# Later stages, an earlier fetch of weights and a shifted unit in a two-layer convolution and attention kernel

## The chip, the cores and the metric

The kernel runs on one core of a Trainium2 chip. The metric is the device time of one execution in microseconds (us), lower is better; the time of a kernel is the median of its runs. Beside the timed runs there is one profiled execution, from which the trace and the profile come.

## The reference

Two layers act on an image batch `x` of shape (2, 256, 64, 64), all in float32. In short:

```
# layer 0
q, k, v = 1x1 convolutions of x, 8 heads of 32 channels, 4096 tokens an image
fuse    = softmax(q k^T / sqrt(32)) v              # per head, 4096 x 4096
hybrid  = Wf [x, fuse] + bf                        # 1x1 convolution
x       = hybrid * m + x * (1 - m)                 # m: mask, resized bilinearly
# layer 1
x = x * sigmoid(relu(x ca_w1 + b) ca_w2 + b)       # channel gate
x = x + window_attention(x)                        # 8x8 windows, 4 heads of 64
x = shuffle of the channels (4 groups)
y = relu(bn(conv7x7(x, groups=64)))                # 256 -> 64 channels
y = bn(conv7x7(y, groups=64))                      # 64 -> 256 channels
out = x * sigmoid(y)
```

The full attention of layer 0 is most of the arithmetic. The two grouped 7x7 convolutions need whole rows around each pixel, so they can begin for an image only when enough of its rows have come out of layer 1's window attention.

## The kernel before

**Preparation.** A first part projects q, k and v chunk by chunk and puts them into DRAM. It is not touched.

**Attention in slots.** `pipeline` walks over 1024 slots: image `b` (2), chunk `c` of 512 query tokens (8), half of the heads `g` (2) and block `m` of 128 keys (32). A chunk is therefore 64 slots. In slot `i` the loop emits the scores of slot `i + 2` (TensorE, L643), which ScalarE turns into exponentials in a tile `e` (L656, eight buffers, `EB = 8`), and the products of slot `i` with v (TensorE, L695). VectorE adds every `e` tile into a running sum (L701), from which the softmax denominators come later. A tile `e` is free again when its product and its sum are done.

**Denominators.** At the last slot of each half, all chunks before the last two ("folded" chunks) have their sums added up across partitions by accumulating DMAs on GpSimd's queue (`fold`, L673). Some slots after the end of a chunk, `at(delay, action)` emits: a few matmuls (`dna`, L729) and a copy (`inva`, L736), a reciprocal on VectorE (L756), a store of the reciprocals to DRAM (`invs`, L741), a broadcast load of them to all partitions (`rda`, L748) and last the multiplication of the attention's result (`fa`, L762). For a folded chunk these stand 10, 11, 11, 11 and 17 slots behind the chunk's last slot; for the last two chunks 8, 9, 9, 9 and 15.

**Stages.** The rest of layers 0 and 1 up to the convolutions is the generator `stage(b, c)`, in 13 pieces. Each piece is emitted after a slot whose number is a multiple of four, while the attention of the next chunk runs. The pieces, in order: `hy` (L529, the 1x1 convolution over x and over `fa`), `ca1` and `ca2` (channel sums and gate), projection `qk0`, window scores `sc0`, `qk1`, `sc1`, `v`, the normalising, `pt` (transposes), `o`, `op` (output projection), and last `xo` (L1009) with the row stores `xs` (L1024) into DRAM, which go through GpSimd's queue, behind the folds and ahead of the next chunk's `invs`. The stage is put into the list of stages 17 slots behind a folded chunk (29 for the very first), so `hy` comes after slot 16 of the next chunk, in program order right behind `fa`; 16 slots behind an unfolded one.

**The tail.** After the last slot the last chunk's denominators and stage remain, and the convolutions. The convolutions are the generator `convolve`: 26 items, each a unit `u` of channels (16) and one or both images. An item has a first half `conv1` (L1093) and a second half `conv2` (L1118), then `gate` (L1145, VectorE) and twelve stores to the output per image (L1172), spread over the queues of GpSimd and SyncE. Rows `xea`, `xla` come by `load_rows` (L1072) and weights `wa` by `load_w` (L1065), both on SyncE's queue. Weights of units 1 to 8 live in the eight `e` buffers, so a load waits until attention has given the buffer back. The first nine items belong to image 0 and can be run before the last stage is done; item 9 is the first one that needs rows of image 1 and so the last stage's `xs`. `convolve` yields after each half, and the tail's loop advances it by one half wherever a piece of the last stage ends with `yield True`:

```
        while stages:
            if run_stages():
                next(conv)
```

So the order of TensorE's work in the tail is written out by the yields. In the kernel before it is: conv1(0), conv1(1), dna, conv2(0), conv1(2), conv2(1), hy, conv1(3), ca1, ca2, conv2(2), qk0, conv1(4), sc0, qk1, conv2(3), sc1, v, conv1(5), pt, conv2(4), o, conv1(6), op, conv2(5), conv1(7), conv2(6), conv1(8), conv2(7), conv1(9), and then halves alone. Nothing is planned by costs[...].

Of the kernel before, what the change touches and what calls it, by code (L numbers as in the profile page):

```python
# [17 lines left out]
B, C, H, W = 2, 256, 64, 64  # L18
# [4 lines left out]
NCHUNK = N // CH  # L23
# [7 lines left out]
EB = 8  # L31
DN = 8
# [25 lines left out]
def conv_seq_kernel(ctx: ExitStack, tc: tile.TileContext, a, out):  # L58
# [14 lines left out]
    def psum2(name):  # L73
        return ps["pair"].tile([P, 2, CH], F32, tag="s", name=name)
# [458 lines left out]
    def pipeline(arm, shifted, pools):  # L533
# [20 lines left out]
        es, acc, first, totals = {}, {}, {}, {}  # L554
        now = [0]
        later = deque()
        stages = deque()

        def at(delay, action):
            later.append((now[0] + delay, action))  # L560
# [13 lines left out]
        def load_q(b, c):  # L574
            q = qp.tile([P, KC, CH], F32, tag="q", name=f"q{arm}_{b}_{c}")
            nc.sync.dma_start(q, q_s[b, c].rearrange("p (g n) -> p g n", g=KC))
            qts[b, c] = q
# [188 lines left out]
        def stage(b, c):  # L766
# [45 lines left out]
                    )  # L812
            gt = gp.tile([P, half], F32, tag="g", name=f"g{tag}")
            nc.scalar.activation(gt, s[:, 0, 0:half], AF.Relu, bias=cb1)
            yield
            s = psum2(f"ca2{tag}")
            for oc in range(KC):
                for h in range(2):
# [219 lines left out]
        def convolve():  # L1038
# [17 lines left out]
            def load_w(u):  # L1056
                if u >= NU:
                    return
                n = 2 * 32 * UW
                if u == 0:  # L1060
                    t = cpool.tile([P, n], F32, tag="w0", name=f"w{arm}{u}")
                else:
                    t = ep.tile([P, HG, CH], F32, tag="e", name=f"w{arm}{u}")
                    t = t.rearrange("p h n -> p (h n)")[:, 0:n]
                nc.sync.dma_start(t, w_s[u])  # L1065
                ws[u] = t

            def load_x(k):
                u, images = items[k]
                x = xs[k] = early[k % 4] if k < EARLY else xcs[(k - EARLY) % len(xcs)]  # L1070
                for i, b in enumerate(images):
                    nc.sync.dma_start(  # L1072
                        x[:, nb * i : nb * i + nb].rearrange("p n g w -> p n (g w)"),
                        x_s[b, :, :, UG * u : UG * u + UG, :].rearrange("n p g w -> p n (g w)"),
                    )

            def load_rows(k):

                while len(xs) < min(k + 1, len(items)) and (
                    staged or B - 1 not in items[len(xs)][1]  # L1080
                ):
                    load_x(len(xs))

            def conv1(k):
                if k >= len(items):
                    return
                u, images = items[k]
                n = nb * len(images)
                w = ws[u][:, 0 : 32 * UW].rearrange("p (m g d) -> p g d m", g=UG, d=KS)
                s = psum1(f"c1{arm}{k}")  # L1090
                for d in range(KS):
                    for j in range(4):
                        nc.tensor.matmul(  # L1093
                            s[32 * j : 32 * j + 32, 0 : n * W],
                            w[:, j, d, :],
                            xs[k][:, 0:n, j, d : d + W],
                            start=(d == 0),
                            stop=(d == KS - 1),
                        )
                y = ys[k] = ycs[k % 2]  # L1100
                nc.scalar.activation(
                    y[:, 0:n, PAD : PAD + W],
                    s[:, 0 : n * W].rearrange("p (n x) -> p n x", x=W),
                    AF.Relu,
                    bias=cbias1[:, u : u + 1],
                )
# [34 lines left out]
            def gate(k, zs):  # L1141
                u, images = items[k]
                for m in range(len(images)):
                    x = xs[k][:, nb * m : nb * m + nb, :, PAD : PAD + W]
                    nc.vector.tensor_mul(zs[m], zs[m], x.rearrange("p n g x -> p g n x"))  # L1145

            def store(k, zs):
                u, images = items[k]
                engines = (nc.gpsimd, nc.gpsimd, nc.sync)
                if k == len(items) - 1:  # L1150
                    engines = (nc.scalar, nc.sync)
                elif k == len(items) - 2:
                    engines = (nc.scalar, nc.sync, nc.sync)
                elif k == len(items) - 3:
                    engines = (nc.gpsimd, nc.sync, nc.sync)
                elif len(images) == 2:
                    engines = (nc.gpsimd, nc.sync)
                stores = 0
                for m, b in enumerate(images):
                    for n, (x0, r0, r1) in enumerate(BLOCKS):  # L1160
                        for i in range(4):
                            p = 32 * i + 1 - x0
                            stores += 1
                            args = (
                                dst[b, i, r0:r1, UG * u : UG * u + UG, :],
                                zs[m][p + r0 : p + r1, :, n, :],
                            )
                            eng = engines[stores % len(engines)]
                            if eng is nc.scalar:
                                held.append(lambda a=args: nc.scalar.dma_start(*a))  # L1170
                            else:
                                eng.dma_start(*args)  # L1172
                if k == len(items) - 1:
                    while held:
                        held.popleft()()

            def more():
                if staged and not xcs:

                    for n in range(3):  # L1180
                        t = ep.tile([P, HG, CH], F32, tag="sum", name=f"xl{arm}{n}", bufs=3)
                        t = t.rearrange("p h n -> p (h n)")[:, 0 : B * nb * UG * WP]
                        xcs.append(t.rearrange("p (n g w) -> p n g w", n=B * nb, g=UG, w=WP))
                    xcs.append(pool.tile([P, B * nb, UG, WP], F32, name=f"xl{arm}3"))
                    for n in (2, 0):
                        xcs.append(room[:, n : n + 2].rearrange("p k n g w -> p (k n) g w"))
                    load_rows(EARLY)
                return bool(xcs)
# [2 lines left out]
            load_rows(3)  # L1191
            load_w(0)
            pool = yield
            for _ in range(4):
                load_w(weights.popleft())
            conv1(0)
            yield
            for k, (u, images) in enumerate(items):
                while len(xs) <= k + 1 < len(items):
                    if not more():  # L1200
                        yield
                conv1(k + 1)
                yield
                more()
                z = conv2(k)
                yield
                more()
                gate(k, z)
                if xcs:
                    load_rows(min(len(xs) + (k >= EARLY - 1), k + len(xcs)))  # L1210
                elif k + 4 < EARLY:
                    load_rows(k + 4)
                store(k, z)

                if weights and (weights[0] <= 1 + EB or k >= EARLY + 4):
                    load_w(weights.popleft())

# [8 lines left out]
        def run_stages():  # L1226
            while stages:
                waits = next(stages[0], stages)
                if waits is not stages:
                    return waits  # L1230
                stages.popleft()
# [10 lines left out]
        for i, (b, c, g, m) in enumerate(slots):  # L1242
            now[0] = i
            if (b, c, g, m) == (B - 1, NCHUNK - 1, 0, 12):
                for _ in banded:
                    pass
                conv = convolve()
                next(conv)
            if m % PB == 0:
                load_piece(i // PB + AHEAD)  # L1250
            if g == KC - 1 and m == 0:
                nxt = (b, c + 1) if c + 1 < NCHUNK else (b + 1, 0)
                if nxt[0] < B:
                    load_q(*nxt)
            rest = scores(i + 2) if i + 2 < len(slots) else None
            products(i)
            if rest:
                rest()
            if g == KC - 1 and m == NMB - 1:
                late = EB + 4 if (b, c) == (0, 0) else 0  # L1260
                at(DN + 8 + ((b, c) < (B - 1, NCHUNK - 2)) + late, lambda b=b, c=c: stages.append(stage(b, c)))
            run_later()
            if i % 5 == 1:
                next(banded, None)
            if i % 4 == 0:
                run_stages()
# [102 lines left out]
```

## Time and profile before

| what | value |
|---|---|
| median of 3 runs (lowest, highest) | 2900.6 us (2898.96, 2902.66) |
| profiled execution, its own time | 2911.19 us |
| its span, from first to last instruction | 2909.3 us |
| TensorE busy | 2863.8 us, 98% of the span |
| VectorE busy | 2435.4 us, 84% |
| ScalarE busy | 2455.3 us, 84% |
| GpSimd busy | 569.1 us, 20% |
| mean share of the DMA engines in use | q1 28.6%, q0 12.2% |
| last product of attention | about 2690 us |
| last matmul of the last convolution | about 2895 us |

A view of the waits names for every engine and line what it waited for, how long in total, how often, and the longest single wait. The chain is the path of work and releases that ended last. A timeline lists the instructions of one engine with start, duration and count, and the idle time before them in brackets. "issue" stands where an engine was idle and no semaphore explains it.

### The profile page before, as it was taken

What the parts mean: (1) busy time and instruction counts of PE and PEld (TensorE: products, weight loads), DVE (VectorE), ACT (ScalarE), POOL (GpSimd) and SP (SyncE); (2) the same over time, 40 slices, a digit from 0 to 9 for tenths busy, and PEclk for the clock granted to TensorE, in tenths of its full rate; (3) what the DMA queues carried; (4) which work ended last, traced back from release to release, by engine and by line L of the source; (5) the groups of instructions that cost most, each with busy time, mean ns of one, the idle gap of its engine ahead of it and who ended that gap; (6) DMA issues with size and microseconds to landing.
All of it is one profiled execution on the core that took longest, in us unless ns stands there. A gap on an engine that the chain in (4) does not pass through costs nothing.

```text
span 2909.3 us, 85471 instructions
## 1 busy us (share of the span) xinstructions
PE 2863.8 (98%) x37002; PEld 827.4 (28%) x37002; DVE 2435.4 (84%) x1344; ACT 2455.3 (84%) x4145; POOL 569.1 (20%) x937
## 2 busy tenths in 40 slices
PE   8999999999999999999999999999999999999998
PEld 3551122222222222222222222222222222222675
DVE  4249999899999999998999999999999899999211
ACT  5569989898989898989989898989899898989433
POOL 8111111111111212121111011111212110000476
PEclk9999999999999999999999999999999999999999
DMA  8545433433253434353333324343435342232565
GB/s 253 209 163 189 146 89 76 94 82 89 65 101 79 105 77 105 79 95 86 82 92 79 88 68 98 78 97 78 100 82 97 82 88 78 67 113 88 137 197 134
DMA packets 245690, 305.65 MB, mean 105 GB/s; under 512 B 121208, under 2 KB 137772, under 8 KB 245048
## 3 DMA queue, kind: packets, MB, share of 16 engines
q1 hardware_dynamic: 200068, 231.51, 28.6%
q0 software_dynamic: 40464, 65.79, 12.2%
q8 instruction: 293, 4.80, 0.7%
q10 hardware_dynamic: 4772, 2.79, 0.3%
q14 instruction: 93, 0.76, 0.1%
HBM read 221.88 MB, written 66.39 MB: 99 GB/s over the span
## 4 chain that ended last, share of the span: by engine, by line
PE 89%; DMA 4%; POOL 2%; issue 2%; DVE 2%; ACT 1%; ACTq 0%; POOLq 0%; DVEq 0%
PE sa L643 34%; PE ava L695 33%; PE qka L529 4%; PE hya L529 3%; PE c1a L1093 2%; PE vwa L529 2%; PE opa L529 2%; PE c2a L1118 2%; PE v L475 2%; PE q L438 2%; PE k L438 1%; DMA xs<-xo 1%; POOL out_dram L1172 1%; DMA invs<-inva 1%; DMA folda<-suma 1%
## 5 line engine op out<-in xcount | busy, mean ns | idle before, releaser
L656 ACT ACTIVATE ea<-sa 128x512 f32<-128x512 f32 (+1 forms) x3072 | 2037.0, 746 | 51.5 <-PE sa L643 24.5
L643 PE MATMUL sa<-qa,ka 32*64 32x512 f32 x16384 | 1147.5, 613 | 1.5 <-ACT vst L483 1.2
L701 DVE TENSOR_TENSOR suma<-suma,ea 128x2048 f32<-128x2048 f32 x480 | 1096.4, 2284 | 5.7 <-ACT ea L656 0.5
L695 PE MATMUL ava<-ea,va 128*32 128x512 f32 x8192 | 1091.8, 605 | 1.0
L701 DVE TENSOR_TENSOR odda<-odda,ea 128x2048 f32<-128x2048 f32 x420 | 958.4, 2282 | 45.9 <-ACT ea L656 45.8
L673 POOL DMA_DIRECT2D folda<-suma x336 | 235.7, 903 | 1669.6 <-DVE suma L703 981.6
L643 PEld LDWEIGHTS sa<-qa,ka 32*64 32x64 f32 x16384 | 242.4, 129 | 786.2 <-ACT ea L656 716.3
L695 PEld LDWEIGHTS ava<-ea,va 128*32 128x32 f32 x8192 | 161.6, 108 | 834.9 <-issue 805.4
L1172 POOL DMA_DIRECT2D out_dram<-za x212 | 119.7, 573 | 58.7 <-DVE za L1145 31.8
L701 DVE TENSOR_TENSOR suma<-ea,ea 128x2048 f32<-128x2048 f32 x32 | 73.2, 2286 | 58.9 <-ACT ea L656 58.9
L529 PE MATMUL qka<-ua,qkv_w 128*32 128x512 f32 x1024 | 115.8, 592 | 0.1
L785 ACT ACTIVATE ta<-hya,bf 128x512 f32<-128x512 f32 x32 | 20.3, 684 | 100.6 <-PE hya L529 94.6
L1024 POOL DMA_DIRECT2D xs<-xo x94 | 72.3, 1058 | 139.6 <-DVE xo L1009 137.4
L457 DVE TENSOR_REDUCE top<-sq 128x128 f32<-128x2048 f32 x16 | 36.6, 2285 | 74.8 <-ACT sq L451 74.8
L741 POOL DMA_DIRECT2D invs<-inva x62 | 34.2, 560 | 296.9 <-DVE inva L756 296.0
L1118 PE MATMUL c2a<-yca,wa 32*64 32x192 f32 (+1 forms) x2912 | 84.4, 367 | 3.7 <-issue 3.4
L903 ACT ACTIVATE ewa<-ewa,mxwa 128x64 f32<-128x64 f32 x256 | 85.3, 346 | 1.5 <-DVE mxwa L894 1.5
L1129 ACT ACTIVATE za<-c2a 128x384 f32<-128x384 f32 x64 | 27.8, 487 | 66.0 <-PE c2a L1118 38.5
L789 DVE TENSOR_TENSOR ta<-ta,mca 128x512 f32<-128x512 f32 x32 | 22.0, 688 | 67.1 <-ACT ta L785 67.1
L861 ACT ACTIVATE qka<-qka,qkv_b 128x512 f32<-128x512 f32 x64 | 40.2, 680 | 39.5 <-PE qka L529 39.5
L1118 PEld LDWEIGHTS c2a<-yca,wa 32*64 32x64 f32 x2912 | 67.5, 191 | 21.1 <-issue 13.9
L1145 DVE TENSOR_TENSOR za<-za,xla 128x768 f32<-128x768 f32 x16 | 15.3, 959 | 65.2 <-DMA out_dram<-za 36.4
(143 smaller groups left out, 1721.3 us busy)
## 6 DMA issues: line engine op xcount, KB each, us to landing
ka<-ks SPq DMA_DIRECT2D x256, 256.0 KB
va<-vs SPq DMA_DIRECT2D x256, 256.0 KB
wa<-ws SPq DMA_DIRECT2D x17, 896.0 KB
ws<-zeros SPq DMA_DIRECT2D x16, 896.0 KB
folda<-suma POOLq DMA_DIRECT2D x224, 64.0 KB, 3.2
folda<-suma POOLq DMA_DIRECT2D x112, 128.0 KB, 3.8
xs<-xo POOLq DMA_DIRECT2D x78, 140.0 KB, 8.1
x<-in_x_dram SPq DMA_DIRECT2D x16, 512.0 KB
```

The lines of the kernel that those rows point to most:

```text
L438: nc.tensor.matmul(s[:, g, :], w[:, kc, g * P : (g + 1) * P], rhs, start=(kc == 0), stop=(kc == KC - 1),)
L475: nc.tensor.matmul(sv[:, m, :], xs0[i][:, kc, m * P : (m + 1) * P], wv[:, kc, :], start=(kc == 0), stop=(kc == KC - 1),)
L529: nc.tensor.matmul(out[o : o + 32], weights[:, o : o + 32], x, start=start, stop=stop)
L643: nc.tensor.matmul(heads[j][o], k[r, cols][:, o], q[r, g, :], start=True, stop=not shifted)
L656: nc.scalar.activation(e[:, h, :], tile, AF.Exp, scale=SCALE0)
L673: nc.gpsimd.dma_start(dst[p : p + rows], total[rows * k : rows * k + rows, h, :], accum_op=ALU.add if k else ALU.bypass,)
L695: nc.tensor.matmul(av[r, :], v[:, m % PB, r], e[:, j, :], start=start, stop=stop)
L701: nc.vector.tensor_add(total, first.pop(m % chains, total), e)
L903: nc.scalar.activation(e[:, n, :], e[:, n, :], AF.Exp, bias=mx[:, n : n + 1], accum_out=rs[:, n : n + 1],)
L1024: eng.dma_start(x_s[b, n, p + r0 : p + r1].rearrange("r g w -> g r w"), xo[64 * h : 64 * h + 64, oc, r0 - WS * c : r1 - WS * c, :],)
L1118: nc.tensor.matmul(tiles[j // 2][o, j % 2, 0 : n * W], w[r, d, o], y[r, 0:n, d : d + W], start=(d == 0), stop=(d == KS - 1),)
L1172: eng.dma_start(*args)
```

## The change

There are four edits. The stages of folded chunks are put into the list 21 slots behind their chunk instead of 17, which is one step of four slots later (`hy` after slot 20, `xs` after slot 4 of the chunk after next); the first chunk keeps its 29 slots and the last two their 16. When attention ends, six weights are asked for instead of four (units 1 to 6), and the two are left out of items 0 and 1's turn. Item 0 now ends with its gate: its request for rows of item 4, its stores and its weight are not emitted there; the rows and the stores follow in item 1's turn, after the piece `hy` of the last stage, and item 1 asks for weight 7. Last, the piece `ca1` yields `True`, so that in the tail one half of a unit comes between `ca1` and `ca2`; all later halves move up by one place, and conv2(5) now stands ahead of `op`.

```
@@ stage
             nc.scalar.activation(gt, s[:, 0, 0:half], AF.Relu, bias=cb1)
-            yield
+            yield True
             s = psum2(f"ca2{tag}")
@@ convolve
             pool = yield
-            for _ in range(4):
+            for _ in range(6):
                 load_w(weights.popleft())
             conv1(0)
...
                 gate(k, z)
+                if k == 0:
+                    first = z
+                    continue
                 if xcs:
                     load_rows(min(len(xs) + (k >= EARLY - 1), k + len(xcs)))
                 elif k + 4 < EARLY:
                     load_rows(k + 4)
+                if k == 1:
+                    store(0, first)
                 store(k, z)
-
                 if weights and (weights[0] <= 1 + EB or k >= EARLY + 4):
                     load_w(weights.popleft())
@@ the slots' loop
             if g == KC - 1 and m == NMB - 1:
-                late = EB + 4 if (b, c) == (0, 0) else 0
-                at(DN + 8 + ((b, c) < (B - 1, NCHUNK - 2)) + late, lambda b=b, c=c: stages.append(stage(b, c)))
+                late = 5 if (b, c) < (B - 1, NCHUNK - 2) else 0
+                if (b, c) == (0, 0):
+                    late = EB + 5
+                at(DN + 8 + late, lambda b=b, c=c: stages.append(stage(b, c)))
             run_later()
```

The order of TensorE's work in the tail becomes: hy, conv1(3), ca1, conv2(2), ca2, conv1(4), qk0, conv2(3), sc0, qk1, conv1(5), sc1, v, conv2(4), pt, conv1(6), o, conv2(5), op, conv1(7), conv2(6), conv1(8), conv2(7), conv1(9).

## The prediction

> **What bounds the kernel.** I read the page first, then the waits of TensorE, the waits and timelines of VectorE, GpSimd and SyncE around one chunk's reciprocals, and the tail's timelines. The page:
>
> ```profile
> span 2909.3 us, 85471 instructions
> ...
> PE 2863.8 (98%) x37002; PEld 827.4 (28%) x37002; DVE 2435.4 (84%) x1344; ACT 2455.3 (84%) x4145; POOL 569.1 (20%) x937
> ```
>
> TensorE (PE) is the bound. An edit pays only where it takes idle time from PE or from the few us after its last matmul (2895). The waits of PE over the whole span, in part:
>
> ```profile
> PE c1a L1093 <- issue: 5.6, 3, 3.3
> ...
> PE hya L529 <- DVE fa L762: 5.4, 4, 1.6
> PE dna L729 <- DMA folda<-suma: 3.4, 2, 2.0
> PE c2a L1118 <- issue: 3.4, 3, 1.5
> ...
> PE ca2a L820 <- ACT ga L814: 0.6, 1, 0.6
> ```
>
> Four waits of hy on `fa` are what the moved stages touch: three in the attention (0.81, 1.64 and 1.53 us, at 833, 1308 and 2257) and 1.46 in the tail. The two of `dna` belong to the first chunk (337 to 340), which keeps its place. All "issue" waits lie in the tail. Why `fa` is late, for the chunk at 833, on POOL's timeline and VectorE's:
>
> ```profile
> 809.57 0.70 POOL L1024 DMA_DIRECT2D xs<-xo  x1 [0.92 <-DMA folda<-suma]
> 818.26 2.20 POOL L741 DMA_DIRECT2D invs<-inva  x4 [8.00 <-DVE inva L756]
> 826.89 2.00 POOL L748 DMA_DIRECT2D rda<-invs  x4 [6.43 <-DMA invs<-inva]
> ```
>
> ```profile
> 832.19 1.22 DVE L762 TENSOR_TENSOR fa<-fa,rda 128x1024 f32<-128x1024 f32 x1 [1.07 <-DMA rda<-invs]
> ```
>
> The reciprocals were issued 8.0 us after the last of eight `xs` stores and took over 5 us to land; in the next chunk that gap is 9.27 us and the load follows sooner (2.31 idle). The tail, on PE's timeline and by stretches (PE busy first, the clock and then DMA share and GB/s last):
>
> ```profile
> 2705.23 3.64 PE L529 MATMUL hya<-xa,WfT 128*32 128x512 f32 x32
> 2710.33 3.64 PE L529 MATMUL hya<-fa,WfT 128*32 128x512 f32 x32 [1.46 <-DVE fa L762]
> ...
> 2746.56 0.54 PE L1093 MATMUL c1a<-xea,wa 128*32 128x192 f32 x2
> 2750.45 3.75 PE L1093 MATMUL c1a<-xea,wa 128*32 128x192 f32 x50 [3.35 <-issue]
> ```
>
> ```profile
> 2745.00:2747.00 2.00, 2.00 (x93) 1.46 (x81) 0.00 (x0) 1.43 (x3) 1.05 (x2) 1.00 0.94 364
> 2747.00:2750.00 3.00, 0.10 (x1) 0.00 (x0) 0.96 (x1) 1.44 (x3) 1.43 (x3) 1.00 0.38 91
> 2750.00:2753.40 3.40, 2.95 (x40) 1.86 (x44) 0.00 (x0) 0.00 (x0) 3.09 (x6) 0.50 1.01 284
> ```
>
> conv1(6) stops after two matmuls for 3.35 us, just after 2 us of DMA at 364 GB/s, and then runs at half clock.
>
> [...] its instruction queue q8 has 293 packets with 4.80 MB, 16 KB each. [...] The stretch above shows 0.50 for 3.4 us, which costs 1.7 us.
>
> **The change, part by part.**
>
> *A. Stages four slots later.* No instruction is added. Four slots are 4 x 2.04 = 8.2 us of PE (sixteen sa 1.04 and eight ava 1.00), and the three waits are at most 1.64: they go, **-3.98**. What else moves: `op` (3.43) goes from slot 60 to the next chunk's slot 0, still ahead of dna, so PE reaches dna at the same moment. On POOL the order fold, xs, invs stays. xs now wait for an xo four sums (4 x 2.28 = 9.1 us) later on VectorE, but today they wait for the folds until 803.26 though xo ended at 796.7; with about 1 us won because op no longer precedes slot 63 they begin at about 805, 2 later. The 8.0 us to invs become about 6, so invs may land 2 us later still in the eight chunks with eight xs stores. `fa` then holds VectorE for up to 1.9 (its longest wait in the attention) + 2 = 4 us. The `e` tiles cover this: in the chunk at 991 the sum of slot 17 ended at 1000.67 and ScalarE first needed that buffer at 1009.05, 8.4 us. hy is covered by the 8.2. At nothing, then; beyond 8.2 us of extra delay each further us is PE's, in up to eight chunks. x's load on SyncE goes with hy, 8.2 us later, with a chunk (158 us) to land. The unfolded chunk (1,6) keeps its place, but stage (1,5)'s eight xs (7 us) come 8 us nearer to its invs (2556.6); they start then at about 2544 and are issued by 2551, so 5 us remain. Its fa ended at 2571.6 and hy's half began at 2573.3: 1.7 us hide it. Ends of A: -4.0 to +10.
>
> *B. Six weights, item 0's rows and stores later.* Weights 5 and 6 wait for the sums of slots 1020 and 1021. VectorE's last six sums take 2.38 each from 2679.93, so they are issued at 2687.1 and 2689.4. SyncE issued weights 1 to 4 in 7.49 us and then nothing until invs at 2699.04; two more at one per 2.4 us are through by about 2695. Behind them on SyncE stand invs and rda, which still have 4 us; without that cover each weight delays the reciprocals by some 2.4. The rows of item 4 (0.38 on SyncE) are still the next thing behind rda on that queue and wait only for gate(0), so they go out at 2703.3 as today. What leaves the time between rda's issue (2702.3 to 2703.8) and its landing (chain: 5.67 us from 2703.31) are eight stores on POOL, four on SyncE and weight 5. rda took 3.1 median in the attention; with 420 KB of rows beside it, 1.2 us at 364 GB/s, it lands at about 2707.6, `fa` (1.23) is done at 2708.9, and hy's first half ends at 2708.87. **-1.3** (0 to -1.46). The eight POOL stores (0.57 each, 4.6 us) now stand behind four xs and ahead of item 1's, which wait for gate(1) at 2718.4: in free time. SyncE's four stand behind the rows of item 5, which wait for gate(1); then eight stores (3.4 us) and weight 7. z has four buffers, the first is needed again near 2745. Nothing there.
>
> *C. One half between ca1 and ca2.* conv2(2) covers ca2's wait on ga: -0.59. But its three ScalarE activations (0.87 for two, 0.85) now precede ca2's tanh (1.26), behind which `ua` on VectorE (1.23) releases qk0: 1.76 + 1.26 + 1.23 + 0.1 = 4.35 after conv2(2), where PE has ca2 1.14 and conv1(4) 2.46. Wait 0.75. Likewise behind conv2(3): 1.76, ewa 0.59, maximum 0.69, exponentials 2.7, qka 1.24 and 0.1 make 7.1, against sc0 0.63, qk1 3.57 and conv1(5) 2.46. Wait 0.45. Net **+0.6** (-0.6 to +1.2).
>
> *D. conv2(5) ahead of op.* op, xo, xs and the rows of image 1 come 2.57 later. Today op ends at 2757.8, these rows are asked for at 2767.45 and land, with 1.2 for 420 KB and 2.3 as invs takes, near 2770.9: 13.1 after op. PE had five halves in between and began conv1(9) 14.2 after op, without a wait. With four (2.46 + 2.57 + 2.46 + 2.57 = 10.1) it waits 3.0. conv1(9) moves by 2.57 + 13.1 - 14.2 = **+1.5** (0 if xs lands as fast as its quickest, 3.2 us instead of about 7; +3.2 if the wait also halves the clock).
>
> *E. Fewer weights amid the halves.* Between 2706 and 2753 SyncE asks for weights 5 to 9, one per item; weight 8 (2743.3) runs just ahead of the 3.35 us stop. Afterwards only 7, 8 and 9 are left there, with items 1 to 3, and none between `v` and op. I take the stop and its half clock as gone: 3.35 + 1.7, **-5.05**. Not shown by the trace: it may be only moved (0), or a second one may come as SyncE sends two items' stores and a weight together (+3.3).
>
> Sum: -3.98 - 1.3 + 0.6 + 1.5 - 5.05 = -8.2, from the span of 2909.3 (own time 2911.2) to 2901.1 (2903.0). The median of the runs is 10.6 below the profiled execution; the same difference gives 2900.6 - 8.2 = 2892.4.
>
> **Rivals.** (1) *The tail gives nothing.* The unprofiled runs are 10.6 us shorter, about what all "issue" waits and the half clock amount to (5.6 + 3.4 + 1.7): perhaps they never have the stop. Then E is 0: -3.2, 2897.4. For it: that coincidence. Against: the DMA load is the program's own. 0.28. (2) *The reciprocals become the bound:* GpSimd's queue carries xs just ahead of invs, rda comes over 8.2 us later than today and fa holds VectorE until the `e` tiles run out. At 10 us, 1.8 in each of eight chunks, 14 lost; with A's 4 not gained and B to E at -4.2, +10: 2911. For it: xs takes 3.2 to 14.1 us to land, and the three late chunks are those with only about 8 us between xs and invs. Against: folds, not xo, time xs today. 0.14. (3) *All tail stops shrink:* traffic falls earlier and the remaining "issue" waits (5.6) halve and more: -13, 2888. 0.08.
>
> **Numbers.** The forecast has 0.50. Its own range is 2889 to 2896 (B, C and D at their ends). A measurement of this kernel tells 0.2%, 5.8 us. Faster takes 0.45 of the forecast, all of (3) and a little of (1): 0.55; slower is (2), 0.14; the rest, 0.31, is the same. The range 2886 to 2904 leaves out most of (2) and the far end of (3).
>
> **What would show it.** A: no wait of hy on fa in the attention; xs issued some 2 us later, invs 6 us behind them, fa's wait on rda longer but no wait of ScalarE for `e`. B: six weights in a row, rda landing by 2708, hy's halves together. C: qk0 and sc1 each idle half a us on `ua` and `qka`. D: an idle PE of 2 to 3 us ahead of conv1(9). E: no stop of over 3 us before op. I am wrong if PE waits on sa or ava in the attention, or if a stop in the tail is as long as before.

## The result, and the profile after

The changed kernel takes 2895.7 us (median of 13 runs, 2889.0 to 2901.43) against 2901.76 (13 runs, 2897.03 to 2907.82) for the kernel before, measured beside it. The ratio is 0.9978, with a 95% interval from 0.997 to 0.9986: 6.4 us less, by the interval 4 to 9. Forecast was a gain of 8.2. The sum held by luck: two of its terms did not, and their errors cancelled.

The page after:

```profile
span 2893.9 us, 85443 instructions
...
PE 2858.3 (99%) x37002; PEld 825.5 (29%) x37002; DVE 2433.2 (84%) x1344; ACT 2458.2 (85%) x4145; POOL 569.9 (20%) x937
```

The span fell by 15.4 us, and the busy time of TensorE (PE), with the same 37002 matmuls, by 5.5: part of what went was not idle time but matmuls that took longer. The waits of PE after, in part:

```profile
PE c2a L1118 <- issue: 2.8, 3, 1.4
PE c1a L1093 <- DMA xla<-xs: 2.4, 1, 2.4
...
PE c1a L1093 <- issue: 1.3, 1, 1.3
PE hya L529 <- DVE fa L762: 1.2, 1, 1.2
...
PE qka L529 <- DVE ua L838: 0.7, 1, 0.7
...
PE sca L882 <- ACT qka L861: 0.5, 1, 0.5
```

hy's four waits have become one, and the stop of 3.35 us at conv1(6) is gone; one of 0.88 us is left in the half ahead of op. New are the three that the prediction named: qk0 on `ua` (0.7), sc1 on `qka` (0.5), conv1(9) on its rows (2.4). Cut at the `dna` of the 1st, 2nd, 15th and 16th chunk, at the last matmul and at the end, the two traces have these stretches (us):

| stretch | before | after | difference |
|---|---|---|---|
| start to dna 1 | 335.6 | 334.5 | -1.1 |
| to dna 2 | 162.9 | 158.8 | -4.1 |
| to dna 15 (13 chunks) | 2051.3 | 2043.2 | -8.1 |
| to dna 16 | 146.0 | 147.4 | +1.4 |
| to the last matmul (the tail) | 199.4 | 195.7 | -3.7 |
| to the end | 14.2 | 14.3 | +0.1 |

The first two rows (-5.2) are the first chunk, which the change doesn't touch: its `dna` waited 3.4 us for the folds before and 1.1 after, and the other traces with the same code up to there reach dna 2 after 493.5 to 499.7 us. 8.1 are the folded chunks. For the chunk at 813, GpSimd's timeline after:

```profile
798.86 5.62 POOL L1024 DMA_DIRECT2D xs<-xo  x8 [4.59 <-DVE xo L1009]
813.53 2.19 POOL L741 DMA_DIRECT2D invs<-inva  x4 [9.05 <-DVE inva L756]
821.01 2.01 POOL L748 DMA_DIRECT2D rda<-invs  x4 [5.28 <-DMA invs<-inva]
```

`rda` still waits 5.3 us for `invs` to land, but hy now comes four slots later. The three chunks in which it waited took 158.75, 159.58 and 159.48 us instead of 157.74: 4.6 of the 8.1 (3.98 of waits and what follows them). The rest is in the time of a chunk in which nothing waits, 157.74 us before and 157.47 after: 13 times 0.27, 3.5 us. The place is slot 32. PE's timeline of the kernel before (start, duration, then engine, line, operation, tiles and count) has there the short piece sc0 and the scores behind it:

```profile
1190.65 0.69 PE L882 MATMUL sca<-qka 64*64 64x64 f32 x32
1191.28 1.39 PE L643 MATMUL sa<-qa,ka 32*64 32x512 f32 x16
```

and ScalarE's at the same time:

```profile
1189.01 0.59 ACT L708 COPY fa<-ava 128x512 f32<-128x512 f32 x1
1189.47 2.53 ACT L656 ACTIVATE ea<-sa 128x512 f32<-128x512 f32 x4
1191.82 0.66 ACT L890 COPY ewa<-sca 128x512 f32<-128x512 f32 x1
```

The half chunk's copy of `f` (0.59) and sc0's copy (0.66) both come there, while PE adds only the 0.69 of sc0; the scores take 1.39 instead of 1.11. From the starts of successive scores, the two slots there take 2.80 and 2.32 us, against 2.67 and 2.04 at sc1, the same piece at slot 40: 0.41 more. On PE's timeline after, sc0 stands at slot 36, and these are the scores behind it:

```profile
1192.16 1.17 PE L643 MATMUL sa<-qa,ka 32*64 32x512 f32 x16
```

What now shares a slot with a copy of `f` is qk0 (3.6) at 32 and op at 0, at 0.08 each (5.55 against 5.47), and 0.06 stays with sc0. At slot 0 the copy alone had cost 0.08 before. So -0.41 + 0.08 + 0.06 = -0.27.

### The profile page after: what moved, and what is told of

It reads as the page before. It is cut to its first block, busy times and chain, and to the rows that moved or that the text cites. A ratio compares the mean times of both kernels' runs of the same rounds, so it can differ in the third digit from the quotient of the medians.

```text
span 2893.9 us, 85443 instructions
## 1 busy us (share of the span) xinstructions
PE 2858.3 (99%) x37002; PEld 825.5 (29%) x37002; DVE 2433.2 (84%) x1344; ACT 2458.2 (85%) x4145; POOL 569.9 (20%) x937
## 4 chain that ended last, share of the span: by engine, by line
PE 93%; DMA 2%; issue 1%; DVE 1%; ACT 1%; POOL 1%; SPq 0%; DVEq 0%; POOLq 0%; ACTq 0%
PE sa L643 36%; PE ava L695 34%; PE qka L529 4%; PE hya L529 4%; PE c2a L1118 2%; PE c1a L1093 2%; PE vwa L529 2%; PE opa L529 2%; PE v L475 2%; PE q L438 1%; PE k L438 1%; PE sca L882 1%; PE pta L957 1%; PE oa L976 1%; PE ca2a L820 1%
## 5 line engine op out<-in xcount | busy, mean ns | idle before, releaser
L1024 POOL DMA_DIRECT2D xs<-xo x94 | 67.2, 722 | 201.6 <-DVE xo L1009 200.5
L701 DVE TENSOR_TENSOR odda<-ea,ea 128x2048 f32<-128x2048 f32 x30 | 68.6, 2288 | 37.3 <-ACT ea L656 37.3
L894 DVE TENSOR_REDUCE mxwa<-ewa 128x8 f32<-128x512 f32 x32 | 21.9, 686 | 61.9 <-ACT ewa L890 61.9
```

What stands on the lines that cost most here:

```text
L701: nc.vector.tensor_add(total, first.pop(m % chains, total), e)
L1024: eng.dma_start(x_s[b, n, p + r0 : p + r1].rearrange("r g w -> g r w"), xo[64 * h : 64 * h + 64, oc, r0 - WS * c : r1 - WS * c, :],)
```

## The experiments

Each ratio is to the kernel before on the same chip in the same hours; that kernel's own median was 2901.8 to 2912.0 us in the four sessions, so kernels are compared by ratio, and the us column is the ratio times the median of before. Theory 1 is that the gain in the timed runs lies in the attention, while the tail's edits about cancel; each expectation names the theories that it sets apart.

| kernel | ratio, 95% interval | us, interval |
|---|---|---|
| the change | 0.9978, 0.997 to 0.9986 | -6.4, -8.7 to -4.1 |
| stages_only | 0.9971, 0.996 to 0.9983 | -8.4, -11.6 to -4.9 |
| tail_only | 1.0001, 0.9991 to 1.001 | +0.3, -2.6 to +2.9 |
| no_half_unit | 0.9971, 0.9961 to 0.998 | -8.4, -11.3 to -5.8 |
| hy_stays_rest_later | 1.0019, 1.0012 to 1.0027 | +5.5, +3.5 to +7.8 |
| eight_later | 0.9999, 0.999 to 1.0007 | -0.3, -2.9 to +2.0 |
| first_chunk_later | 0.9954, 0.994 to 0.9968 | -13.4, -17.5 to -9.3 |
| three_more_halves | 1.0005, 0.9997 to 1.0013 | +1.5, -0.9 to +3.8 |
| weights_only | 0.9991, 0.9981 to 1.0 | -2.6, -5.5 to 0 |
| half_unit_only | 1.0003, 0.9993 to 1.0014 | +0.9, -2.0 to +4.1 |
| sc0_four_later | 1.0016, 1.0007 to 1.0024 | +4.7, +2.0 to +7.0 |

**stages_only**: the kernel before with A alone.

```
-                late = EB + 4 if (b, c) == (0, 0) else 0
-                at(DN + 8 + ((b, c) < (B - 1, NCHUNK - 2)) + late, ...)
+                late = 5 if (b, c) < (B - 1, NCHUNK - 2) else 0
+                if (b, c) == (0, 0):
+                    late = EB + 5
+                at(DN + 8 + late, ...)
```

> The kernel before with the stages of folded chunks four slots later and nothing else. Theory 1 (the attention gives it all: 4.0 us of waits of hy on fa, and 14 x 0.27 us because no short piece stands at slot 32 any more, less about 1.2 us for the hy of the unfolded chunk 14): 6 to 7 us faster than before, and the chunk's period falls from 157.74 to 157.47 us. Theory 2 (the prediction: hy's waits 4.0, the rest from the tail): 4 us faster or less, period unchanged outside hy's waits.

Measured -8.4 us, more than the change itself, though the two intervals overlap. Its trace has the same 2043.2 for the 13 chunks. **tail_only** is its counterpart, the changed kernel with these lines taken back:

```
-                late = 5 if (b, c) < (B - 1, NCHUNK - 2) else 0
...
+                late = EB + 4 if (b, c) == (0, 0) else 0
+                at(DN + 8 + ((b, c) < (B - 1, NCHUNK - 2)) + late, ...)
```

> The changed kernel with the stages put back to 17 slots: six weights, item 0's rows and stores later, half a unit between the channel sums. Theory 1: within 2 us of before, since the waits won and lost in the tail cancel. Theory 2: 4 us faster, from the stop of 3.35 us and its half clock and hy's wait in the tail.

Measured +0.3: the tail's edits together give nothing that can be told from zero. Its trace has 157.74 again for a chunk in which nothing waits.

**hy_stays_rest_later** splits A. From ca1 on the pieces move by four slots, hy keeps its own:

```
@@ stage, behind hy
             yield True
+            if (0, 0) < (b, c) < (B - 1, NCHUNK - 2):
+                yield
```

> The kernel before with an empty piece behind hy in the folded chunks after the first: hy stays behind slot 16, all later pieces move by four slots, so sc0 leaves slot 32. Theory 1: the period of a chunk falls by 0.27 us to 157.47 outside hy's waits; hy's waits stay or grow to 4 to 15 us, because the row stores move towards the reciprocals: 0 to 3.5 us faster than before, or slower if the waits grow. Theory 2 (no cost at slot 32): period 157.74, no faster than before.

Measured +5.5. The slots from 21 on take exactly what they take after the change, with the 0.27 gained; but the slot in which hy falls takes 9.70 us or more in every chunk instead of 8.91, since hy now waits each time (0.59 us or more). **sc0_four_later** tests slot 32 by itself: hy to qk0 stay, and sc0 and all behind it come four slots later.

```
@@ stage, ahead of the first window scores
             project_out(0, project(0))
             yield True
+            if (0, 0) < (b, c) < (B - 1, NCHUNK - 2):
+                yield
             window_scores(0)
```

> The kernel before with one empty step ahead of the first window scores in the stages of the folded chunks but the first: hy to qk0 keep their slots (16 to 28), slot 32 has no piece, sc0 comes at slot 36 and op at slot 0 of the next chunk. Theory (sc0 at slot 32 meets the copy of f on ScalarE): the period of a chunk falls from 157.74 to about 157.45, 13 chunks or -3.7 us, a ratio of 0.9987; hy's waits on fa stay (1.7 to 4.0 us). Rival (the gain comes from a long piece at slot 32, in which ScalarE catches up): the period stays at 157.7 and the ratio at 1.0.

The first half of this came. With nothing at slot 32 and sc0 at 36, the three slots concerned take 2.17, 2.04 and 2.67 us, so the 0.41 is down to the 0.13 that the copy of `f` costs alone: that sc0 stands at slot 32 is confirmed as the cause. That it is the copy of `f` which it meets there is read from ScalarE's timeline. But the ratio rose, which neither theory expected. From PE's waits in this kernel:

```profile
PE hya L529 <- DVE fa L762: 15.1, 13, 3.4
```

hy waits in 13 chunks. VectorE's timeline tells why, in a chunk where `rda` is in time. First that of the kernel before:

```profile
1147.53 1.22 DVE L762 TENSOR_TENSOR fa<-fa,rda 128x1024 f32<-128x1024 f32 x1
```

Then that of sc0_four_later:

```profile
1121.88 1.29 DVE L1011 TENSOR_TENSOR xo<-ya,ua 128x512 f32<-128x512 f32 x2
...
1150.31 1.21 DVE L762 TENSOR_TENSOR fa<-fa,rda 128x1024 f32<-128x1024 f32 x1
```

A sum starts 2.20 us after the one before it, and a slot is 2.04: between pieces VectorE falls behind. With op at slot 0, `xo` (1.29) stands behind three of the chunk's sums instead of ahead of them all. hy's first half starts at 1145.54 before and at 1147.37 here, so `fa` starts 1.99 us after it before and 2.94 here, and hy's second half is 0.59 late. Both splits come to 158.28 a chunk. That it is `xo` is read from the timelines; no run moved `xo` alone. But A's two gains are not independent: what moves sc0 off slot 32 moves op to slot 0, and only hy's own four slots pay for that.

**eight_later** doubles A's step: stages_only with `late = 9`.

> The kernel before with the folded stages eight slots later instead of four (hy behind slot 24), the tail untouched. Theory 1 (two terms, hy's wait on fa and what shares ScalarE with the copies of f at slots 0 and 32): hy waits nowhere in the attention, but the short pieces ca2 and o now fall on slots 32 and 0, where ScalarE has the copy of f and a copy of its own of 1.25 us; the period of a chunk comes out between 157.5 and 158.1, against 157.47 with four slots: 0 to +9 us over 14 chunks against four slots later. Theory 2 (only hy's wait on fa mattered): the same 2895 us as with four slots later. Theory 3 (the reciprocals become the bound, since xs now stand three slots, about 6 us, ahead of invs): fa's waits on rda grow by up to 8 us and TensorE waits on sa or ava: 2905 or more.

Measured -0.3: all of A's gain is lost again. Theory 3's mechanism is what happened, though not its size: 2905 or more would be a ratio above 1.001, and the time itself lies within theory 1's range. Theory 1's mechanism, as far as it concerns ca2 and o, did not show: they stand beside the copies of `f`, and their slots lose only 0.13 and 0.08, no more than the copy alone, 157.53 a chunk. Why sc0's slots lose three times as much isn't settled. Two chunks take 163.65 and 162.25, a third 159.48. The first of these on GpSimd's timeline of eight_later:

```profile
1286.05 5.62 POOL L1024 DMA_DIRECT2D xs<-xo  x8 [11.86 <-DVE xo L1009]
1292.02 0.57 POOL L741 DMA_DIRECT2D invs<-inva  x1 [0.35 <-DVE inva L756]
...
1306.68 2.00 POOL L748 DMA_DIRECT2D rda<-invs  x4 [8.11 <-DMA invs<-inva]
```

`fa` on VectorE's:

```profile
1315.44 1.23 DVE L762 TENSOR_TENSOR fa<-fa,rda 128x1024 f32<-128x1024 f32 x1 [10.68 <-DMA rda<-invs]
```

and PE a little later:

```profile
1319.61 1.96 PE L643 MATMUL sa<-qa,ka 32*64 32x512 f32 x4 [1.72 <-ACT ea L656]
```

`xs` are issued straight ahead of `invs`, these go out one by one, and `fa` can start 23.8 us after the last of `xs` was issued (1315.44 against 1291.67). Until then it has held VectorE for 10.7 us, the `e` tiles run out, ScalarE stops 3.13 us, and PE 1.72. By stretches of the granted clock (PE busy first; PEclk, DMA share and GB/s last) PE then runs 6.8 us at 0.51 and 0.50 of its clock:

```profile
1319.60:1323.00 3.40, 3.39 (x12) 0.68 (x16) 3.40 (x2) 3.20 (x5) 0.00 (x0) 0.51 0.00 0
1323.00:1326.40 3.40, 3.40 (x20) 0.79 (x16) 3.40 (x3) 0.16 (x1) 0.00 (x0) 0.50 0.00 0
```

This is rival (2)'s mechanism, four slots further on than the prediction had placed it, and with PE stopped in two of the chunks instead of eight.

**no_half_unit** is the changed kernel without the half unit, so without C and D.

```
@@ stage, behind ca1
-            yield True
+            yield
```

> The changed kernel without the half unit between ca1 and ca2. Theory 1: the waits on ua (0.70), qka (0.45) and the rows of image 1 (2.43) go and the wait on ga (0.59) comes back, while conv2(5) again stands behind op: 1 to 3 us faster than the changed kernel, 7 to 9 faster than before. Theory 2 (the half unit also keeps the stop of instructions away): as the changed kernel or up to 4 us slower, with a stop of about 3 us at conv1(6).

Measured -8.4, 2 us below the change, in line with +2.1 for C and D, though the intervals overlap. Against stages_only, which has A alone, B and E show nothing: both give -8.4. **weights_only** and **half_unit_only** put B and the `yield True` into the kernel before, one each.

```
weights_only
-            for _ in range(4):
+            for _ in range(6):
...      (and item 0's rows and stores in item 1's turn)
half_unit_only, behind ca1
-            yield
+            yield True
```

> The kernel before with the tail's second edit alone: six weights at attention's end, item 0's rows and stores behind hy in item 1's turn; stages and half unit as before. Steps B and E as predicted: the stop of 3.3 us with its half clock at conv1(6) goes, and rda comes 1.3 us sooner: -6.4 us, a ratio of 0.9978. Rival 1 (E gives nothing): -1.3 us or less, 0.9995 to 1.0. In the trace the stop at conv1(6) is 0 to 2.5 us long under both, since no trace with these weights has had a longer one.

> The kernel before with the half unit between ca1 and ca2 alone; weights, stores and stages as before. Steps C and D as predicted: +0.6 and +1.5 to +3.2, so +2 to +4 us, a ratio of 1.0007 to 1.0013, with a wait of 2 to 3 us of conv1(9) on its rows. If it is the order of the weights that ends the stop at conv1(6), a stop of 3.3 to 3.7 us is still there. Rival: the stop's end belongs to the halves that moved up, not to the weights; then no stop of over 2.5 us at conv1(6), and about -2 us.

B stands here for the tail's second edit, the earlier weights and later stores, of which E is the hoped-for effect on the stop. weights_only comes to -2.6, nearer to rival 1's -1.3 than to -6.4, which lies just outside its interval; half_unit_only to +0.9, with conv1(9) 2.44 us late as forecast. The stop at conv1(6) doesn't belong to the weights alone. PE's timeline in half_unit_only, with the old order of weights, in the half ahead of op:

```profile
2749.74 1.26 PE L1118 MATMUL c2a<-yca,wa 32*64 32x192 f32 x38 [1.60 <-issue]
```

In the half just ahead of op, the traces have a stop of 3.35, 3.41, 3.69, 3.26 and 2.99 us with neither edit (before, stages_only, hy_stays_rest_later, eight_later, sc0_four_later), of 0.82, 0.70 and 2.44 with the weights alone (weights_only, no_half_unit, first_chunk_later), of 1.60 with the half alone, and of 0.88 and 1.01 with both (the change, tail_only). Either edit shortens it; neither is its one cause.

**three_more_halves** tests D: in the changed kernel three more pieces are followed by a half.

```
             window_scores(0)
-            yield
+            yield True
...      (the same behind normalise(0) and normalise(1))
```

> The changed kernel with three more halves of the early items ahead of op: one behind sc0, one behind each of the two normalising pieces, so that conv1(7), conv2(6) and conv1(8) also come before op. Theory of step D (the way from op over xs and the rows of image 1 to conv1(9) takes about 13 us, and halves behind op hide it): op comes 7.5 us later, conv2(7) alone is left behind it, and conv1(9) waits about 10 us on its rows: +6 to +8 us against the changed kernel, 2902 to 2904, if nothing else in the tail shrinks; the waits of qk0 on ua and sc1 on qka go up by 0 to 1 us. Rival (the halves only fill idle TensorE, and image 1 is not on the path): no slower than the changed kernel, 2893 to 2896.

PE's timeline of this kernel from op on:

```profile
2756.57 3.62 PE L529 MATMUL opa<-ota,out_w 128*32 128x512 f32 x32
2760.11 2.64 PE L1118 MATMUL c2a<-yca,wa 32*64 32x192 f32 x112
2774.09 4.03 PE L1093 MATMUL c1a<-xla,wa 128*32 128x192 f32 x56 [11.34 <-DMA xla<-xs]
```

13.9 us lie between the end of op and conv1(9), 13.8 in half_unit_only and 12.4 after the change: the way over `xo`, `xs` and the rows sets conv1(9), and halves ahead of op are taken from what hides it. Ratio 1.0005 against 0.9978 for the change: 7.8 us more between two sessions, of the size expected (6 to 8).

**first_chunk_later** is no_half_unit with two edits against the waits left in the attention, in the slots' loop and where the denominators are asked for:

```
+                if (b, c) == (0, 0):
+                    wait, late = wait + 4, late - 4
...
-                late = 5 if (b, c) < (B - 1, NCHUNK - 2) else 0
+                late = 5 if (b, c) < (B - 1, NCHUNK - 3) else int((b, c) == (B - 1, NCHUNK - 3))
```

> The changed kernel without the half unit between ca1 and ca2, with the very first chunk's denominators four slots later (its stage keeps its place) and with the stage of the last folded chunk back at its 17 slots. If the waits left in the attention count in the timed runs as in the profile: the first chunk's dna no longer waits on the folds (1.1 to 3.4 us, and 1.7 more where the clock halves), the unfolded chunk's hy does not wait on fa (0.9 to 1.2), and sc0 meets the copy of f once (+0.27): 2 to 5 us below the same kernel without these two edits, about 2890 to 2893. If not: 2894 to 2896, the same as without them.

Measured -13.4, from five runs: below both kernels, and its interval (0.994 to 0.9968) ends under that of the change (0.997 to 0.9986). Neither wait is in its trace any more, though two of hy's have come in their place (1.13 in the first chunk, 0.60 in the last folded one). Against no_half_unit, whose interval touches its own, the two edits are not resolved, and its trace shows no gain there: it reaches dna 2 after 495.3 us, that of no_half_unit after 495.2.

## Why the prediction was right, and where it was wrong

**The sum** of -8.2 met -6.4, inside the forecast's range. It is made of A -4.0, B -1.3, C and D +2.1, E -5.05; the runs show A -8.4 and all of the tail +0.3, where the sum had -4.2 for B to E.

**A was put at half of what it is.** "No instruction is added", and so nothing but hy's waits was priced: the step that failed is "*At nothing, then*" for the rest of the stage. It asked what the moved pieces delay, and not what they meet in their new slots and had met in the old ones; sc0's old place cost 0.27 net in each chunk, 3.5 us, and stood in the trace of before as scores of 1.39 beside many of 1.11. The waits themselves were mis-sized, coming from one execution: in the four traces with the old places and a tail edited or not (before, tail_only, weights_only, half_unit_only) the 13 chunks take 2051.3, 2049.0, 2055.8 and 2053.9, with waits of 1.7 to 6.8 us; in four with the new places 2043.2 three times (the change, stages_only, no_half_unit) and 2043.8 (three_more_halves). The difference of the means, 9.2, less some 1 us at the unfolded chunk, comes near the 8.4 of stages_only. That chunk's cover, put at 1.7 us, was too thin: hy waits 0.6 to 1.2 there, and 2.36 in three_more_halves. The feared delay behind `xs` didn't come: they begin 14.7 us ahead of `invs` in the chunk shown (15.0 before), are issued in 5.6 us instead of 7, and leave 9.05 us where 6 had been forecast; PE has no new wait for `e`.

**B** came in the trace after: six weights in a row, hy's halves together, no wait of 1.46. But that wait, too, was a sample. In the tail hy waits 1.46, 0.94, 0.85, 0.39 and twice not at all in the six traces with the old order of weights (before, eight_later, hy_stays_rest_later, half_unit_only; stages_only, sc0_four_later), and 1.11, 0.86 and four times not at all in the six with the new one (first_chunk_later, tail_only; the others): 0.3 less on the mean, and no run shows the -1.3. **C** held to a tenth in the trace: 0.70 and 0.45 us were measured where 0.75 and 0.45 had been worked out, and ca2's 0.59 went. **D** was right in kind, and at its upper end: 2.43 us of wait where 3.0 were expected, and then conv1(9) at a granted clock of 0.50 (from 2756.36 on, for 3.41 us), its 56 matmuls in 4.16 us instead of 2.54, on PE's timeline after:

```profile
2756.32 4.16 PE L1093 MATMUL c1a<-xla,wa 128*32 128x192 f32 x56 [2.43 <-DMA xla<-xs]
```

In the timed runs C and D together are worth +0.9 (half_unit_only) to +2.0 (the change against no_half_unit); +2.1 lies within both intervals, though in half_unit_only the stop shrank too.

**E** is the other step that failed: "*I take the stop and its half clock as gone*". Ahead of op the trace after has this left of them, at a granted clock of 1.00:

```profile
2739.38 0.97 PE L1118 MATMUL c2a<-yca,wa 32*64 32x192 f32 x31 [0.88 <-issue]
```

Still -5.05 isn't in the time: B and E together give -2.6 (0 to -5.5) in weights_only, where -6.35 had been forecast; how this divides between them isn't shown. Two things were wrong. The reason, a weight just ahead of the stop, isn't borne out: in half_unit_only a weight is asked for 1.5 us ahead of the stop (2746.67 against 2748.14), and the stop is half as long. And the stop gets shorter rather than going: the three traces with the weights alone keep 0.70 to 2.44 us of it. Their tail, from the last `dna` to the last matmul, takes 192.6 us on the mean; it takes 199.4, 194.3, 194.5, 200.5 and 196.3 in the traces with neither edit, 197.0 on the mean. The difference of 4.4 is no more than the scatter of these five traces.

The long stop of before ends at 2750.45 us, 1.31 us after the end of a packet of queue q8, whose kind is instruction on the page; the other stops of this kind in the tails of before and after end alike (the last section has the figures). That packet begins at 2748.18, after the stretch in which 94% of the DMA engines' time was taken (2745 to 2747). Whether this load held it up is not shown.

**Rival (1)** had the nearest size for the tail: +0.8 without E, and +0.3 was measured. Its reason, that executions without the profiler never have the stop, is open. The coincidence that it named went: in the other eleven kernels the profiled execution lies between 6.7 below and 6.8 above the median of its kernel, on the mean at it, so that of before was a long one, and its 10.6 was no constant to carry over. The span fell by 15.4 us where the median fell by 6.4. But in the five traces with a stop of about 3 us the profiled execution lies 1.1 to 10.6 above its median, and in the other seven from 6.7 below to 0.7 above, but for three_more_halves (3.6 above). So many of the timed executions may lack the long stop, and then E had little to win in them; a timed run leaves no trace that could tell. **Rival (2)** has the right mechanism, and its point of decision lies between four and eight slots.

## What to carry to other kernels

When a piece of work is moved past others, price what it meets on every engine in its new place and what it met in the old one: a chunk in which nothing waits, timed slot by slot, shows it at once. A margin moved from one hand to the other has an end on both sides: here four slots cover a late transfer and eight make its store collide with the next one. A wait seen in one execution is a sample; look at the same stretch in several traces before its length goes into a sum.

## What the runs showed of the hardware

**The clock.** Half clock was seen behind waits of PE of well under the 3.35 us of the long stop, but not behind each of them. Behind waits of 2.43 us (conv1(9) in the change, granted clock 0.50) and 2.44 (the same in half_unit_only) 56 matmuls took 4.16 and 4.19 us, against 2.54 for the conv1 that comes next in the change's trace. In weights_only hy's 32 matmuls took 5.34 us behind a wait of 2.25 and 3.64 behind one of 2.64. From PE's timeline of weights_only:

```profile
1306.77 5.34 PE L529 MATMUL hya<-fa,WfT 128*32 128x512 f32 x32 [2.25 <-DVE fa L762]
...
2257.76 3.64 PE L529 MATMUL hya<-fa,WfT 128*32 128x512 f32 x32 [2.64 <-DVE fa L762]
```

and the stretches around these two waits, cut where its own clock record has them (PE busy first; PEclk, DMA share and GB/s last):

```profile
1304.53:1307.94 3.41, 1.17 (x12) 0.42 (x16) 1.23 (x1) 0.00 (x0) 0.00 (x0) 1.00 0.00 1
1307.94:1311.35 3.41, 3.41 (x20) 0.87 (x16) 0.00 (x0) 0.00 (x0) 0.00 (x0) 0.50 0.00 0
2253.44:2256.86 3.42, 1.68 (x16) 0.26 (x8) 0.52 (x2) 0.00 (x0) 0.00 (x0) 1.00 0.39 120
2256.86:2260.27 3.41, 2.51 (x24) 0.81 (x28) 0.84 (x1) 0.00 (x0) 0.00 (x0) 1.00 0.00 0
```

The shorter wait falls into one stretch and leaves PE busy for 0.34 of it, and the next has a clock of 0.50; the longer one is split over two, with 0.49 left in the first, and the clock is 1.00 in both. In the traces of before and after, the stretches ahead of a half clock, up to the last matmul, have PE busy for 0.24 and 0.15 (from 336.76 and 2746.57 us, before) and for 0.29 (from 2752.94, after). With the two traces cut every 3.413 us at the same places, no other stretch from 25 us to the last matmul has less than 0.52. The half clocks begin at 340.18, 2749.99 and 2900.17 us before, which lie 706 and 44 times 3.413 us apart, and at 2756.36 and 2882.65 after, 37 times.

With a third wait of 1.89 in the trace of weights_only the waits of hy come to 6.8 us, and their three chunks are 9.1 us longer than one without (159.84, 161.89 and 160.59 against 157.74). The prediction had put hy's waits in the attention at their length alone, and a half clock of 1.7 us behind the stop of 3.35.

**The instructions.** In the tails of before and after PE stops ten times for 0.3 us or more without a semaphore that explains it ("issue"). All ten stops end 1.30 to 1.58 us after the end of a packet of queue q8, the page's queue of kind instruction (293 packets, 16 KB each); of times spread evenly over the two tails, about one in twenty lies so.
